# A four-stage fused kernel: copies and grid products regrouped in the attention stage, and a new end of the last image

## The chip, the cores and the metric

The kernel runs on one core of a Trainium2 chip. The metric is the device time of one execution in microseconds (us), and lower is better. Three executions of the kernel before took 2770.07, 2771.0 and 2774.91 us; their median is 2771.0 us.

## The reference, cut to what matters

Four layers are applied one after the other to `x`, which holds 8 images of 512 rows and 512 columns, all in float32:

```python
# layer 0: a grid step; Af, Bf are x times coefficient grids, _grad/_grad2 are differences of neighbours
x = maximum(f + (-gradv_Af + gradvv_Bf * 0.5) * dt, 0)
# layer 1: attention with 16 heads of 32, a bias [8,16,512,512] and a key mask, then an MLP of 2048
x = _ln(src) * (1 + scale) + shift
q, k, v = x @ Wq + bq, x @ Wk + bk, x @ Wv + bv
probs = softmax(where(mask, -inf, q/sqrt(32) @ k.T + attention_bias))
x = x + (probs @ v @ Wo + bo);  h = _ln(x) * g2 + beta2
x = x + _gelu2(h @ W1 + b1) @ W2 + b2
# layer 2: one of 8 experts per image
o = gelu(x @ Wi[e] + bi[e]) @ Wo[e] + bo[e] + x
x = (o - mean(o)) * rsqrt(var(o) + 1e-12) * gamma[e] + beta[e]
# layer 3: a rank-32 response, scaled by one number per image
base_act = sigmoid(relu(x.mean(rows) @ gate_w1.T + gate_b1) @ gate_w2.T + gate_b2)
strength = base_act * sigmoid(safety_score)
x = x + strength * ((x @ basis) @ basis.T[:, :32] @ resp_w.T + resp_b + safety_bias)
```

The output is the `x` of the last line.

## The kernel before

The kernel is one program for one core. Nearly every instruction is put down through `pin`, which keeps the order of the program on its engine, so the order of each engine's queue is the order in which the Python text makes the instructions. An image is held as four tiles of 128 rows: row `4p + r` lies in partition `p` of tile `r`. TensorE is PE below, VectorE DVE, ScalarE ACT, GpSimd POOL.

**Attention stage** (`attention_stage`). The work of an image is cut into 16 units, one for each group `c` of four heads and each tile `r` of query rows; `t = 4c + r` is the step of the unit within its image, and the main loop runs through 128 units. In the step of a unit

- POOL adds the mask to the bias of the next unit (`add_mask`). A small `gate` instruction ahead of it makes it wait until the last grid product of the step before is done,
- PE turns the exponentials of the unit before (`turned`, pair `u` of heads, head `i` of the pair: four transposes into one PSUM tile of the tag `tr`, which has two buffers). DVE copies the tile out where `i` is 0 and ACT where `i` is 1 (L1022 and L1024),
- DVE takes bias minus score and its row minimum (`softmax`, L997) and ACT makes the exponential and its sum (L1002). The four score tiles have one buffer each, so the scores of the next unit wait for this unit's four minima,
- PE does a piece of projection work (`fill`): a block of Q, K or V, or of the output projection. A block is four matmuls in two halves, one after each pair's transposes. In step 9 it is a block of K (`k_block`), and behind it stand the 16 transposes of the next image's input (`x1_in`, four `xtr` tiles of the tag `tr`; DVE copies out tiles 0 and 2, ACT tiles 1 and 3),
- in every second step PE multiplies probabilities and V (`values`), and after the last unit of a head group it transposes the inverse sums (`divide`, tile `rb`, also of the tag `tr`), which ACT copies and DVE multiplies into the context (`ct`),
- DVE does some products of the grid step of a later image, at the end of the step. The dict `GRID` says which: `j` is the step of the grid work, and its image `n` is at `j = t + 8` where `n = b + 1` and at `j = t - 8` where `n = b + 2`. So in each image steps 0 to 8 hold `j = 8` to 16 and steps 8 to 15 hold `j = 0` to 7. What stands in front of a `|` is done ahead of `divide`, the rest behind it. The last image's steps have no grid work, since no image follows.

SP issues the loads of bias tiles (8 buffers) and of grid coefficients (2 and 3 buffers) in the order of the text.

**MLP stage** (`mlp_stage`). Sixteen products `q`: 0 to 7 are the MLP of layer 1, 8 to 15 the experts, each as a Strassen scheme with seven products per level. `run(q, hooks)` counts steps `s`; `hooks` puts other work (loads, the norm and transposes of the next image, the layer-3 end of the image before) in front of step `s`. `second(s, ...)` makes one of the seven products of the second level: 16 matmuls of 128x256 into one PSUM tile, for two tiles of rows at once. The seventh, at steps 52 to 55, gives the left 256 columns of row tiles 2 and 3.

**The end of the last image** (`q = 15`). Row tiles 0 and 1 are complete early: their norm is at hook 49 (`tail_norm`), their transposes in front of steps 51 to 54 (`tail_turn`, L1167 and L1624), and the projection `tail_feats` and the product with gamma (`tail_gamma`, L1604) in front of step 55. After step 55 everything for row tiles 2 and 3 follows: addition, two `bn_stats`, power on POOL, two scalings (L85), eight transposes in pairs with ACT copies, the rank-32 projection `pf` alternating with the gate product `pg`, `h1` in two DVE instructions, then `po` for four row tiles (weights `rw`, then `ones` times the bias row `rb`), then `strength` (`pz`, a sigmoid on ACT, a product on DVE), then four sums on DVE (`tail_add`, L1683) and two stores from SP (L1688).

Of the kernel before, what the change touches and what calls it, by code (L numbers as in the profile page):

```python
# [544 lines left out]
def attention_stage(  # L545
# [13 lines left out]
    with ExitStack() as ctx:  # L559
# [85 lines left out]
            )  # L645
            qs[b, c] = t

        def k_block(b, c, tag="m"):
            pr = ps.tile([P, S], F32, name=f"pk_{b}_{c}", tag=tag)
            half = block(  # L650
                pr, lambda k: w["Wk"][:, k, c * P : (c + 1) * P], lambda k: x1s[b, k]
            )
            yield half(0)
            yield half(1)
            t = pp.tile([P, S], F32, name=f"kt_{b}_{c}", tag="kt")
            pin(nc.scalar.activation(t, pr, AF.Identity, bias=bqk[:, 1, c : c + 1]))
            ks[b, c] = t

        def v_block(b, m, tag="m", bufs=1):
            pr = ps.tile([P, D], F32, name=f"pv_{b}_{m}", tag=tag, bufs=bufs)  # L660
# [98 lines left out]
        def grid_op(n, op):  # L759
# [59 lines left out]


        GRID = {
            0: "q0 q1", 1: "e0 |", 2: "w0 c0 hh", 3: "C0", 4: "+0 -0", 5: "g0 |", 6: "G0 a0",
            7: "A0 b0 B0", 8: "x0 q2", 9: "e1 | w1 c1", 10: "C1 +1", 11: "-1 g1", 12: "G1 s0",
            13: "a1 | n0 A1 b1", 14: "B1 x1", 15: "s1", 16: "n1",
        }

# [81 lines left out]
        def fill(b, t):  # L908

            n = b + 1  # L910
            jobs = []
            if b == 0:
                if t == 0:
                    homes = (("m", 1), ("tr", 2), ("tr", 2), ("ctx", 1))
                    for m in range(4):
                        jobs.append(v_block(0, m, *homes[m]))
                        jobs.append(grid_early(j) for j in (m + 3,))
                    jobs.append(grid_early(7) for _ in range(1))
                    jobs.append(mask_out(0, r) for r in (2, 3))
                elif t == 2:  # L920
                    jobs.append(add_bv() for _ in range(1))
                elif t in (3, 4, 6, 7):
                    jobs.append(x1_back(0, (3, 4, 6, 7).index(t)) for _ in range(1))
            if t in (0, 4, 8):
                jobs.append(q_block(b, t // 4 + 1))
            elif t in (1, 5, 9):
                jobs.append(k_block(b, t // 4 + 1))
            elif t in (2, 3, 6, 7):
                if b:
                    jobs.append(o_block(b - 1, (2, 3, 6, 7).index(t)))  # L930
            elif n < NB:
                if t == 11:
                    jobs.append(q_block(n, 0))
                elif t == 13:
                    jobs.append(k_block(n, 0))
                else:
                    jobs.append(v_block(n, (10, 12, 14, 15).index(t)))
            if n < NB:
                if t == 9:
                    jobs.append(x1_in(n, c) for c in range(KC))  # L940
                if t in (11, 12, 13, 14):
                    jobs.append(x1_back(n, t - 11) for _ in range(1))
                if t >= 12:
                    jobs.append(load_mask(n, t - 12) for _ in range(1))
            elif t == 8:
                jobs.append(head_stats() for _ in range(1))
            elif t in (10, 11):
                jobs.append(head_norm(r) for r in (2 * t - 20, 2 * t - 19))
            elif t >= 12:
                jobs.append(head_turn(t - 12) for _ in range(1))  # L950
            for j in jobs:
                yield from j
# [55 lines left out]
        def turned(b, c, r, u):  # L1008

            bt = bias.pop((b, c, r, u))  # L1010
            for i in range(2):
                h = 2 * u + i
                if r % 2 == 0:
                    pts[b, c, r // 2, h] = pp.tile(
                        [P, KC, 2, P], F32, name=f"pt_{b}_{c}_{r}_{h}", tag=f"pt{h}", bufs=1
                    )
                pt = pts[b, c, r // 2, h]
                tr = ps.tile([P, KC, P], F32, name=f"tr_{b}_{c}_{r}_{h}", tag="tr", bufs=2)
                for k in range(KC):
                    tp(tr[:, k, :], bt[:, i, k * P : (k + 1) * P])  # L1020
                if i == 0:
                    pin(nc.vector.tensor_copy(pt[:, :, r % 2, :], tr))  # L1022
                else:
                    pin(nc.scalar.copy(pt[:, :, r % 2, :], tr))  # L1024
# [111 lines left out]
def mlp_stage(tc, a, small, xp, io, wo8, x1d, ident, eidx, sigs, layernorm, rstd_of, phalf, wl3, g2, b1, first):  # L1136
# [19 lines left out]
    with ExitStack() as ctx:  # L1156
# [297 lines left out]
        def run(q, hooks):  # L1454
# [119 lines left out]
            add(yu, p7, yu)  # L1574
            x_add(1, 1, yu)
            x_add(1, 0, yu)
            p4 = second(52, lambda g: act_quad(g, 1, 1), b(1, 0))
            x_add(1, 0, p4)

        def t13(q, g):  # L1580

# [46 lines left out]
                )  # L1628
                t["ys"][c] = y

        def tail_feats(q, rows):
            ys = outs[q]["ys"]
            pf = ps.tile([P, P], F32, name=f"pf_{q}_{rows[0]}", tag="tr")
            for c in range(KC):
                for i, r in enumerate(rows):
                    mm(
                        pf[r * RK : (r + 1) * RK, :], wl3[:, c, :], ys[c][:, i, :],
                        c == 0, c == KC - 1,
                    )
            m = slice(rows[0] * RK, (rows[-1] + 1) * RK)  # L1640
            pin(nc.vector.tensor_copy(outs[q]["ft"][m, :], pf[m, :]))

        def gate(q):

            pooled = outs[q]["pooled"]
            if len(pooled) > 1:
                add(pooled[0], pooled[0], pooled[1])
            pg = ps.tile([P, 1], F32, name=f"pg_{q}", tag="tr")
            for c in range(KC):
                mm(pg, gw1[:, c, :], pooled[0][:, c : c + 1], c == 0, c == KC - 1)  # L1650
            h1 = small.tile([P, 1], F32, name=f"h1_{q}", tag="h1")
            pin(nc.vector.tensor_scalar(h1, pg, 1.0 / S, gb1, ALU.mult, ALU.add))
            pin(nc.vector.tensor_scalar(h1, h1, 0.0, None, ALU.max))
            outs[q]["h1"] = h1
# [13 lines left out]
            gadd(x, x, beta[:, None, :].to_broadcast([P, R, D]))  # L1668

        def tail_sum(q, r):  # L1670
            last = q == NQ - 1
            ft, m = outs[q]["ft"], slice(r * RK, (r + 1) * RK)
            po = outs[q]["po", r] = ps.tile(
                [P, D], F32, name=f"po_{q}_{r}", tag="u", bufs=6
            )
            mm(po, ft[m, :], rw[m, :], True, not last)
            if last:
                mm(po, ones[m, :], rb[m, :], False, True)

        def tail_add(q, r):  # L1680
            x, t = xs[q], outs[q]
# [5 lines left out]
            if r % 2:  # L1687
                nc.sync.dma_start(  # L1688
                    a["out"][q - NB].rearrange("(p r) f -> p r f", r=R)[:, r - 1 : r + 1, :],
                    x[:, r - 1 : r + 1, :],  # L1690
                )


# [10 lines left out]
        for q in range(NQ):  # L1704
# [50 lines left out]
            if q == NQ - 1:  # L1755
                half = range(0, 2)
                at(hooks, 49, tail_norm, q, half)
                for c in range(KC):
                    at(hooks, 51 + c, tail_turn, q, half, [c])
                at(hooks, 55, tail_feats, q, half)  # L1760
                at(hooks, 55, tail_gamma, q, half)
            run(q, hooks)

        q, half = NQ - 1, range(2, 4)
        x, beta, t = xs[q], extra[q][1][2], outs[NQ - 1]
        gadd(x[:, 0:2, :], x[:, 0:2, :], beta[:, None, :].to_broadcast([P, 2, D]))
        tail_norm(q, half)
        pg = ps.tile([P, 1], F32, name=f"pg_{q}", tag="u", bufs=6)
        for c in range(KC):
            mm(pg, gw1[:, c, :], t["pooled"][0][:, c : c + 1], c == 0, False)  # L1770
        tail_turn(q, half, range(KC))
        tail_gamma(q, half)
        pf = ps.tile([P, P], F32, name=f"pf_{q}_2", tag="u", bufs=6)
        for c in range(KC):
            for i, r in enumerate(half):
                mm(
                    pf[r * RK : (r + 1) * RK, :], wl3[:, c, :], t["ys"][c][:, i, :],
                    c == 0, c == KC - 1,
                )
            mm(pg, gw1[:, c, :], t["pooled"][1][:, c : c + 1], False, c == KC - 1)  # L1780
        m = slice(half[0] * RK, (half[-1] + 1) * RK)
        h1 = small.tile([P, 1], F32, name=f"h1_{q}", tag="h1")
        pin(nc.vector.tensor_copy(t["ft"][m, :], pf[m, :]))
        pin(nc.vector.tensor_scalar(h1, pg, 1.0 / S, gb1, ALU.mult, ALU.add))
        pin(nc.vector.tensor_scalar(h1, h1, 0.0, None, ALU.max))
        t["h1"] = h1
        gadd(x[:, 2:4, :], x[:, 2:4, :], beta[:, None, :].to_broadcast([P, 2, D]))
        for r in range(R):
            tail_sum(q, r)
        strength(q)  # L1790
        for r in range(R):
            tail_add(q, r)


# [86 lines left out]
```

## Time and profile before

| what | value |
|---|---|
| median of three executions | 2771.0 us |
| the profiled execution, by its own time | 2773.14 us |
| its span from the first to the last instruction | 2771.4 us |
| PE, DVE, ACT, POOL busy | 2708.5, 1941.1, 1004.9, 1501.9 us |
| scores of the first unit to those of the last | about 70 to 1104 us |
| first matmul of the MLP stage to the last one of step 55 | 1132 to 2749 us |
| from there to the end of the span | 22.4 us |

A busy PE is not a PE at full speed: ends of matmuls are modelled, and a matmul that waits behind its own first half counts as busy. So times between the same marks of different images are compared below, not busy shares alone. The profiled execution is 2.1 us above the median of the three.

### The profile page before, as it was taken

What the parts mean: (1) busy time and instruction counts of PE and PEld (TensorE: products, weight loads), DVE (VectorE), ACT (ScalarE), POOL (GpSimd) and SP (SyncE); (2) the same over time, 40 slices, a digit from 0 to 9 for tenths busy, and PEclk for the clock granted to TensorE, in tenths of its full rate; (3) what the DMA queues carried; (4) which work ended last, traced back from release to release, by engine and by line L of the source; (5) the groups of instructions that cost most, each with busy time, mean ns of one, the idle gap of its engine ahead of it and who ended that gap; (6) DMA issues with size and microseconds to landing.
All of it is one profiled execution on the core that took longest, in us unless ns stands there. A gap on an engine that the chain in (4) does not pass through costs nothing.

```text
span 2771.4 us, 39819 instructions
## 1 busy us (share of the span) xinstructions
PE 2708.5 (98%) x14662; PEld 2009.6 (73%) x14662; DVE 1941.1 (70%) x3581; ACT 1004.9 (36%) x2137; POOL 1501.9 (54%) x1074
## 2 busy tenths in 40 slices
PE   7899999999999999999999999999999999999998
PEld 4455555555555554788888888888888888888886
DVE  7889898988888756577667666755456566566564
ACT  2566666666666666212111211211121221221221
POOL 3455555555555654466465555655636646646643
PEclk9999999999999999999999999999999999999998
DMA  8665757666666555542542543344133143142120
GB/s 317 234 208 169 240 179 238 192 219 214 193 231 193 162 155 171 173 114 65 160 126 40 154 134 85 101 145 133 58 126 114 58 156 114 58 156 99 59 76 31
DMA packets 190208, 405.27 MB, mean 146 GB/s; under 512 B 24024, under 2 KB 28704, under 8 KB 183742
## 3 DMA queue, kind: packets, MB, share of 16 engines
q1 hardware_dynamic: 186202, 391.97, 42.5%
q0 software_dynamic: 3360, 10.68, 3.1%
q8 instruction: 117, 1.92, 0.3%
q14 instruction: 77, 0.63, 0.1%
q10 hardware_dynamic: 452, 0.07, 0.0%
HBM read 366.97 MB, written 31.50 MB: 144 GB/s over the span
## 4 chain that ended last, share of the span: by engine, by line
PE 86%; DVE 10%; ACT 3%; DMA 1%; issue 1%; SPq 0%; ACTq 0%; POOL 0%; DVEq 0%
PE u L1164 28%; PE y L1164 28%; PE tr L570 7%; PE s L567 4%; PE ctx L567 4%; PE o L567 3%; PE pv L567 3%; PE pq L567 3%; PE pk L567 2%; DVE bt L997 2%; DVE x L687 2%; DVE pt L1022 1%; ACT bt L1002 1%; PE btr L1167 1%; PE ytr L1167 1%
## 5 line engine op out<-in xcount | busy, mean ns | idle before, releaser
L974 POOL TENSOR_TENSOR bt<-bt,mk 128x1024 f32<-128x1024 f32 x256 | 542.7, 2142 | 64.1 <-DMA bt<-in_bias 59.1
L1164 PE MATMUL y<-wo,act 128*128 128x256 f32 x2560 | 573.2, 380 | 0.0
L1164 PEld LDWEIGHTS y<-wo,act 128*128 128x128 f32 x2560 | 481.3, 190 | 70.0 <-issue 6.9
L1002 ACT ACTIVATE bt<-bt,mn 128x512 f32<-128x512 f32 x512 | 365.5, 715 | 112.1 <-DVE mn L997 112.1
L570 PEld LDWEIGHTS tr<-ident,bt 128*128 128x128 f32 x2048 | 228.1, 141 | 169.6 <-issue 116.8
L1164 PE MATMUL u<-bt,wi 128*128 128x256 f32 x1440 | 330.5, 379 | 0.0
L997 DVE CUSTOM_DVE_ANT_0 bt<-s,bt 128x512 f32<-128x512 f32 x512 | 330.5, 683 | 0.0
L1170 DVE TENSOR_TENSOR act<-u,u 128x512 f32<-128x512 f32 x256 | 173.3, 686 | 210.0 <-PE u L1164 132.3
L1164 PEld LDWEIGHTS u<-bt,wi 128*128 128x128 f32 x1440 | 273.5, 190 | 37.2
L570 PE MATMUL tr<-ident,bt 128*128 128x128 f32 x2048 | 280.4, 278 | 20.3 <-DVE pt L1022 8.5
L1022 DVE COPY pt<-tr 128x512 f32<-128x512 f32 x256 | 175.9, 687 | 113.0 <-PE tr L570 112.8
L1164 PE MATMUL u<-tb,ws 128*128 128x256 f32 x1024 | 242.2, 379 | 0.0
L1164 PE MATMUL y<-t,s 128*128 128x256 f32 x1024 | 234.2, 380 | 0.0
L1024 ACT COPY pt<-tr 128x512 f32<-128x512 f32 x256 | 148.3, 579 | 183.3 <-PE tr L570 181.2
L1164 PEld LDWEIGHTS u<-tb,ws 128*128 128x128 f32 x1024 | 194.3, 190 | 26.6 <-DVE tb L1170 0.2
L1173 POOL TENSOR_TENSOR t<-wo,t 128x512 f32<-128x512 f32 x64 | 104.5, 1648 | 200.1 <-PE y L1164 200.0
L1164 PEld LDWEIGHTS y<-t,s 128*128 128x128 f32 x1024 | 191.1, 190 | 24.1
L1484 ACT ACTIVATE act<-act,b 128x512 f32<-128x512 f32 x128 | 82.9, 711 | 292.8 <-DVE act L1170 292.8
L1484 ACT ACTIVATE act<-act,bi 128x512 f32<-128x512 f32 x128 | 83.8, 712 | 282.6 <-DVE act L1170 282.6
L567 PE MATMUL s<-kt,qt 32*128 32x512 f32 x1024 | 171.5, 644 | 2.2 <-DVE mn L997 1.4
L1170 DVE TENSOR_TENSOR x<-y,x 128x512 f32<-128x512 f32 x96 | 64.5, 685 | 154.2 <-PE y L1164 100.3
L1170 DVE TENSOR_TENSOR u<-u,u 128x512 f32<-128x512 f32 x192 | 131.2, 684 | 57.4 <-PE u L1164 57.3
(317 smaller groups left out, 4261.0 us busy)
## 6 DMA issues: line engine op xcount, KB each, us to landing
bt<-in_bias SPq DMA_DIRECT2D x256, 512.0 KB
wo<-in_W SPq DMA_DIRECT2D x32, 1024.0 KB
wi<-in_Wi SPq DMA_DIRECT2D x32, 1024.0 KB
wo<-in_Wo_e SPq DMA_DIRECT2D x32, 1024.0 KB
wi<-in_W SPq DMA_DIRECT2D x28, 1024.0 KB
gq<-coef_q SPq DMA_DIRECT2D x21, 512.0 KB
x1d<-x SPq DMA_DIRECT2D x8, 1024.0 KB
x<-x1d SPq DMA_DIRECT2D x8, 1024.0 KB
```

The lines of the kernel that those rows point to most:

```text
L567: pin(nc.tensor.matmul(out, lhsT=lhsT, rhs=rhs, start=start, stop=stop))
L570: pin(nc.tensor.transpose(out, src, ident))
L687: pin(nc.vector.tensor_tensor(out, x, y, op))
L974: nc.gpsimd.tensor_tensor(bt, bt, mask[b, r][:, None, :].to_broadcast([P, 2, S]), ALU.add)
L997: nc.vector.tensor_tensor_reduce(bt[:, i, :], ss[h], bt[:, i, :], -1.0, 3.0e38, ALU.add, ALU.min, mn)
L1002: nc.scalar.activation(bt[:, i, :], bt[:, i, :], AF.Exp, bias=mn, scale=-1.0, accum_out=sums[b, c, r][:, h : h + 1],)
L1022: pin(nc.vector.tensor_copy(pt[:, :, r % 2, :], tr))
L1024: pin(nc.scalar.copy(pt[:, :, r % 2, :], tr))
L1164: pin(nc.tensor.matmul(out, lhsT=lhsT, rhs=rhs, start=start, stop=stop))
L1170: pin(nc.vector.tensor_tensor(out, x, y, op))
L1173: pin(nc.gpsimd.tensor_tensor(out, x, y, op))
L1484: nc.scalar.activation(acts[g][:, k, :], acts[g][:, k, :], func, bias=bi[:, j : j + 1])
```

## The change

Four edits.

1. *Copies.* In `turned`, the copy of the first head of the first pair moves from DVE to ACT for five of the 16 units of every image: the units 1, 3, 5, 7 and 15, which are turned in steps 2, 4, 6, 8 and in step 0 of the next image.
2. *Grid products.* Six products of `GRID` stand one step earlier (`w0`, `C0`, `+0`, `g0`, `A0` by one step each, and `G0`, now ahead of the `|`). Those of `j = 8` to 16 stay.
3. *Transposes of the next input.* The 16 transposes of step 9 no longer follow the block of K: tiles 0 and 1 stand in front of its fourth matmul, tiles 2 and 3 behind the copy of the block.
4. *The end.* The seventh product of `q = 15` is made row tile by row tile (8 matmuls of one tile, then 8 of the other), and each tile's sum, statistics and scaling follow on their own. The transposes of row tiles 0 and 1 stand in front of steps 51, 52 and 53 (two). `tail_feats` of tiles 0 and 1, the four bias products (`ones`, `rb`) and the first half of `pg` stand behind the last product, ahead of the last transposes. `h1` is one ACT instruction. `pz` stands ahead of the four `rw` products. The last sums: DVE takes row tiles 1 to 3, ACT scales tile 0 and POOL adds it, and each row tile has its own store, three of them from ACT's queue and one from SP's.

```diff
-        def k_block(b, c, tag="m"):
+        def k_block(b, c, tag="m", turn=None):
             pr = ps.tile([P, S], F32, name=f"pk_{b}_{c}", tag=tag)
-            half = block(...)
-            yield half(0)
-            yield half(1)
+            for k in range(KC):
+                mm(pr, w["Wk"][:, k, c * P : (c + 1) * P], x1s[b, k], k == 0, k == KC - 1)
+                if k == 1 or k == (2 if turn else 3):
+                    yield
+                if turn and k == 2:
+                    turn(0)
+                    turn(1)
             t = pp.tile([P, S], F32, name=f"kt_{b}_{c}", tag="kt")
             pin(nc.scalar.activation(t, pr, AF.Identity, bias=bqk[:, 1, c : c + 1]))
+            if turn:
+                turn(2)
+                turn(3)
...
         GRID = {
-            0: "q0 q1", 1: "e0 |", 2: "w0 c0 hh", 3: "C0", 4: "+0 -0", 5: "g0 |", 6: "G0 a0",
-            7: "A0 b0 B0", 8: "x0 q2", 9: "e1 | w1 c1", 10: "C1 +1", 11: "-1 g1", 12: "G1 s0",
+            0: "q0 q1", 1: "e0 | w0", 2: "c0 hh C0", 3: "+0", 4: "-0 g0", 5: "G0 |", 6: "a0 A0",
+            7: "b0 B0", 8: "x0 q2", 9: "e1 | w1 c1", 10: "C1 +1", 11: "-1 g1", 12: "G1 s0",
             13: "a1 | n0 A1 b1", 14: "B1 x1", 15: "s1", 16: "n1",
...
-                jobs.append(k_block(b, t // 4 + 1))
+                turn = (lambda c: x1_in(n, c)) if t == 9 and n < NB else None
+                jobs.append(k_block(b, t // 4 + 1, turn=turn))
...
-                if i == 0:
+                if i == 0 and not (u == 0 and 4 * c + r in (1, 3, 5, 7, 15)):
                     pin(nc.vector.tensor_copy(pt[:, :, r % 2, :], tr))
                 else:
                     pin(nc.scalar.copy(pt[:, :, r % 2, :], tr))
...
+            else:                                    # q == NQ - 1
+                for m in range(2):
+                    y = ps.tile([P, H], F32, name=f"y_{q}_52_{m}", tag="u", bufs=6)
+                    for g in range(NG):
+                        if g % 2 == 0:
+                            go(52 + 2 * m + g // 2)
+                        for i in range(2):
+                            mm(y, act_quad(g, 1, 1)[:, i, m * P : (m + 1) * P],
+                               b(1, 0)(g)[:, i, :], g + i == 0, g + i == NG)
+                    last_row(m, y)
...
+        def last_row(m, y):
+            o = x[:, r, 0:H]
+            add(o, y, o)
+            pin(nc.vector.bn_stats(st, x[:, r, :]))
+            pin(nc.vector.bn_aggr(mv, st))
+            rs = z["rs", r] = rstd_of(mv[:, 1:2], LN_EPS2, 1, "ln2", pin)
+            if m == 0:
+                tail_gamma(q15, [0, 1])
+                scaled()
+                return
+            last_turn(0)
+            tail_feats(q15, range(0, 2), "u", 6)
+            for k in range(R):
+                mm(po, ones[k * RK : (k + 1) * RK, :], rb[k * RK : (k + 1) * RK, :], True, False)
+            for c in range(KC):
+                mm(pg, gw1[:, c, :], t["pooled"][0][:, c : c + 1], c == 0, False)
+            scaled()
+            gadd(x[:, 0:2, :], x[:, 0:2, :], beta[:, None, :].to_broadcast([P, 2, D]))
+            last_turn(1)
+            for c in range(KC):      # ACT: copies of the transposes of tiles 2 and 3, with column sums
...
+            tail_gamma(q15, [2, 3])
+            gadd(x[:, 2:4, :], x[:, 2:4, :], beta[:, None, :].to_broadcast([P, 2, D]))
+            for c in range(KC):      # pf of tiles 2 and 3, and pg, in turn
...
+            pin(nc.scalar.activation(h1, pg, AF.Relu, bias=gb1, scale=1.0 / S))
+            pin(nc.vector.tensor_copy(t["ft"][2 * RK :, :], pf[2 * RK :, :]))
+            strength(q15)
+            for r in range(R):
+                mm(t["po", r], t["ft"][m, :], rw[m, :], False, True)
+            pin(nc.scalar.mul(v, t["po", 0], t["st"]))
+            for r in (1, 2, 3):
+                pin(nc.vector.scalar_tensor_tensor(
+                    x[:, r, :], t["po", r], t["st"], x[:, r, :], ALU.mult, ALU.add))
+                if r == 1:
+                    gadd(x[:, 0, :], x[:, 0, :], v)
+                pin((nc.sync, nc.scalar)[r % 2].dma_start(out[:, r, :], x[:, r, :]))
+                if r == 2:
+                    pin(nc.scalar.dma_start(out[:, 0, :], x[:, 0, :]))
...
                 for c in range(KC):
-                    at(hooks, 51 + c, tail_turn, q, half, [c])
-                at(hooks, 55, tail_feats, q, half)
-                at(hooks, 55, tail_gamma, q, half)
+                    at(hooks, (51, 52, 53, 53)[c], tail_turn, q, half, [c])
```

The lines that stood behind `run(q, hooks)` for the last image are removed; their order is told above.

## The prediction

> **What bounds the kernel now.** I read the page first, then times by step, then the order of time inside single steps.
>
> ```profile
> span 2771.4 us, 39819 instructions
> PE 2708.5 (98%) x14662; PEld 2009.6 (73%) x14662; DVE 1941.1 (70%) x3581; ACT 1004.9 (36%) x2137; POOL 1501.9 (54%) x1074
> PE 86%; DVE 10%; ACT 3%; DMA 1%; issue 1%; SPq 0%; ACTq 0%; POOL 0%; DVEq 0%
> ```
>
> PE is the bound, yet a tenth of the chain that ended last runs through DVE. Where? The MLP stage is shut: from 1400 to 2740 us PE is busy for 1339.77 of 1340 us, and nothing there changes. What is left is the attention stage and the end. Steps 0 to 8 of an image hold the same PE work in every image from image 1 on, but in the last image, 7, they hold no grid products. Their time in image 2 (first line) and in image 7:
>
> ```profile
> 346.77:417.40 70.63, 68.80 (x425) 36.30 (x424) 64.98 (x136) 44.65 (x110) 40.54 (x28) 1.00 0.58 182
> 991.93:1057.92 65.99, 65.99 (x426) 35.41 (x425) 40.44 (x106) 43.14 (x108) 34.02 (x16) 1.00 0.55 175
> ```
>
> The columns are length, then busy time of PE, PEld, DVE, ACT, POOL, then clock and DMA. At the same clock and with the same matmuls the steps with grid products take 4.64 us more. DVE is 92% busy in them, ACT 63%. Only 1.83 us of the 4.64 shows as idle PE; the rest hides in scores that take longer. Step 2 shows how (PE, DVE, ACT, POOL in turn):
>
> ```profile
> 366.32 0.60 PE L570 MATMUL tr<-ident,bt 128*128 128x128 f32 x4
> 367.73 0.66 PE L570 MATMUL tr<-ident,bt 128*128 128x128 f32 x4 [0.81 <-DVE pt L1022]
> 370.04 1.85 PE L567 MATMUL s<-kt,qt 32*128 32x512 f32 x8
> ...
> 365.86 1.22 DVE L687 TENSOR_TENSOR gc<-gc,gf 128x1024 f32<-128x1024 f32 x1
> 366.99 0.69 DVE L1022 COPY pt<-tr 128x512 f32<-128x512 f32 x1
> 371.32 1.36 DVE L687 TENSOR_TENSOR x<-x,gc 128x1024 f32<-128x1024 f32 x1
> ...
> 365.07 0.58 ACT L1024 COPY pt<-tr 128x512 f32<-128x512 f32 x1
> ...
> 367.36 4.23 POOL L974 TENSOR_TENSOR bt<-bt,mk 128x1024 f32<-128x1024 f32 x2
> ```
>
> DVE leaves step 1's grid products at 366.99, only then copies the first transposes, and frees their buffer at 367.7; PE waits 0.81. All minima come later too, and the next scores take 1.85 us instead of 1.14. ACT has been idle since 365.65. In step 6 the wait ends elsewhere:
>
> ```profile
> 399.11 1.26 PE L570 MATMUL tr<-ident,bt 128*128 128x128 f32 x8 [0.70 <-ACT pt L1024]
> 396.98 1.52 ACT L814 ACTIVATE x<-x,gsh,grs 128x512 f32<-128x512 f32 x2
> 398.40 0.56 ACT L1024 COPY pt<-tr 128x512 f32<-128x512 f32 x1
> ```
>
> There ACT itself is late, behind the two norm instructions of the grid work.
>
> **Edit 1, the copies.** Forty DVE copies of 0.69 become ACT copies of 0.57. Per image the stalls against image 7 are, by step (the step's excess, with the scores that open the next step): 0: 0.51 + 0.21; 2: 1.02 + 0.71; 4: 0.18 + 0.21; 6: 1.10 + 0.71; 8: 0.17; in all 4.82. What goes:
> - Step 2: ACT would copy at 365.07 and 365.65 and be done at 366.2, before PE asks at 366.3; the wait is gone. DVE's minima start 0.6 earlier; the second pair's end near where the scores need them, and I leave 0.45 of stall. Gain 1.28.
> - Step 6: both copies stand behind the norms, at 398.40 and 398.96, so the transposes start at 399.1 as before: 0.70 and its refill stay. DVE, a copy lighter, gives the minima 0.6 earlier: gain 0.71.
> - Steps 0, 4 and 8: DVE's wait (0.32 in step 0) and late scores go: 0.72 + 0.39 + 0.17.
>
> Sum 3.27 per image. Behind the moved copies in ACT's queue stand the exponentials, which wait for DVE's minima and come after the copies anyway: no cost. In image 7, where DVE isn't late, the second copy ends 0.2 later; the next transposes come 1.7 later, so nothing, but 0.2 at the stage's very end.
>
> A rule speaks against this. The row: `x<-x,gc` takes 1.36 where the same product takes 1.22 alone, and POOL's mask addition ends at 371.59, 0.27 into it. The Trainium skill (SBUF — State Buffer, Who interferes with whom) says that a DVE instruction with two SBUF inputs and a GpSimd one that reads SBUF block each other fully, whoever comes second. By it a DVE that is early by a copy gains nothing for its products: `gc` is held to 371.59 whenever it comes, since POOL's `gate` ties that addition to the step before. By the row alone it would start earlier for 0.14. I take the block: products then end when they end now, PE arrives up to 1.3 earlier and meets DVE later by that much. Step 3 opens with 1.9 us of `ctx` before its transposes, which absorbs it. If it did not, steps 3 and 7 would give back up to 1.3 and 0.7, leaving 1.3 per image.
>
> **Edit 2, grid products.** Nothing removed; each moved one is 1.2 to 1.36. Step 15 gets one fewer, so step 0 opens with DVE 1.2 less late (in 0.72 above). Step 9 gets `w0` behind `divide`: DVE starts step 10 about 1.2 later, its copy ends at 0.3 before PE needs the buffer, its last minimum about when the scores want it: 0 to 0.1. The `gate` of step 10 waits for `w0`, so POOL's additions move by 1.2 to 2.2, with 3 us to spare before their minima. Coefficient loads keep their SP places; `g0` is issued some 20 us before its new use. Steps 10 to 15 show no stall now. I take 0, bounded by +0.5 and -0.3 per image.
>
> **Edit 3, transposes of the next input.**
>
> ```profile
> 298.27 1.34 PE L570 MATMUL xtr<-ident,x 128*128 128x128 f32 x8 [0.47 <-DVE x L612]
> 299.83 0.66 PE L570 MATMUL rb<-ident,rw 128*128 128x128 f32 x4 [0.22 <-DVE x L612]
> ```
>
> PE reaches `rb` at 299.83. In the new order tile 0 starts at 295.5, when DVE's copy (295.46) frees the buffer; tile 1 ends at 296.5 and matmul 4 at 296.9; DVE is through its minima at 296.67 and copies tile 0 by 297.5; tile 2 follows to 298.1, DVE's next copy ends 298.95, `rb` starts 299.0. ACT does tile 1 right behind its exponentials (297.57), ahead of the K copy. Gain 0.8, for seven images.
>
> Attention: 6 x (3.27 + 0.8) = 24.4 for images 1 to 6. Image 0 has other work in these steps (`x1_back`); its PE waits add up to 8 us from 105 to 231 us, and I give the copies 2 of them, so 2.8 with edit 3. Less 0.2 at the end: 27.0.
>
> **Edit 4, the end.** Stations of before, by PE, DVE and SP:
>
> ```profile
> 2746.99 1.99 PE L1164 MATMUL y<-wo,act 128*128 128x256 f32 x8
> 2753.18 1.27 PE L1167 MATMUL ytr<-ident,x 128*128 128x128 f32 x4 [3.40 <-DVE x L85]
> 2763.78 0.38 PE L1164 MATMUL pz<-h,gw 128*128 128x1 f32 x2
> 2764.76 2.73 DVE L1683 SCALAR_TENSOR_TENSOR x<-po,st,x 128x512 f32<-128x512 f32 x4
> ```
>
> - Last product: the projection of tiles 0 and 1 (1.07 and a wait of 0.2) leaves the front; step 52 still starts at 2740.28. 32 instructions at 0.219 (48 took 10.5) and two transposes give 2748.0 instead of 2748.98. Tile 2's sum starts at 2744.5 and runs beside tile 3's product: 0.4 + 0.69 + 0.2 + 0.2, the gamma product 1.23 (over the power, 0.71), scaling 0.5, done 2747.8.
> - Behind 2748.0 PE does four transposes 0.76, the projection 1.07, four bias products (half of the 3.5 that eight took: 1.75; in separate row groups 1.14, as eight instructions took at 2725.91), `pg` 0.95. DVE needs to 2750.9 for tile 3, so PE is last: transposes at 2751.5 to 2752.3, against 2753.18.
> - Only four transposes, no buffer wait, ACT from 2752.2 at 0.55 each; `pf`/`pg` in the old pitch of 1.09: `pg` ends 2757.3 instead of 2760.41.
> - `h1` on ACT 0.26 (its nearest row is the sigmoid of 128x1), no table load ahead of it in the program. `pz` at 2757.6, since six of the eight `po` passes no longer stand before it: 6.2 earlier than 2763.78. Sum ready 0.98 later as before, 2758.6; `rw` products about 2758.9.
> - Three DVE sums of 0.68 end 2760.95; ACT's scaling (0.58, as its copies) and POOL's addition (1.27 at 2717.26; at most 1.65) end about 2760.9. The last store leaves ACT's queue near 2761.3; the last one now leaves at 2767.54 and the span ends 3.8 later. Gain 6.2 to 6.3.
>
> New here and without a row: stores from ACT's queue, behind POOL's addition (nearest SP's, 0.34 to issue; 0 to 1 us worse). I take 6.3, between 4 and 7.5.
>
> **Sum.** 27.0 + 6.3 = 33.3. The profiled execution would go from 2773.14 to 2739.8; against the median of 2771.0, 2.1 lower, 2737.7. I say 2738.
>
> **Rivals.**
> - *The late DVE comes back in the next step.* The block above takes edit 1 down to 1.3 per image; with 0.8 that is 12.6, image 0 gives 1.5, the end 6: 20, so 2751. For it: DVE is still over 85% busy and its products share the port with 4.2 us of POOL per step. Against: odd steps have 0.6 to 1.1 us of DVE slack each. 0.20.
> - *More stalls go than I count*: steps 2 and 6 fully (1.5 more per image), image 0 by 5 more: 2724. Against: ACT's norms in step 6 stay. 0.10.
> - *The end gains, the attention stage doesn't*, since products moved into step 9 open a new wait there as large as those removed: 2765. 0.04.
> - *ACT becomes the one that PE waits for* (the other side). Forty copies of 0.57 ahead of exponentials; if each holds back the transposes of its step by its whole length and a late exponential holds the next step's too, 46 us come in, the stalls of now stay, and the end gives 6: 2811. It decides where ACT reaches the copies later than DVE does now: in step 2 it is 1.3 us earlier, in step 6 0.6. 0.03.
> - *The edits do not do what they say*: were ACT's copies scheduled elsewhere, 0.01; the order of the changed program shows them in place.
>
> **How the numbers follow.** The likeliest case, 0.62, spans 2732 to 2746. The range adds the first rival to 2751 and some of the second: 2730 to 2752. Differences within 0.2% (5.5 us) can't be told from none here. Faster 0.94, same 0.03, slower 0.03.
>
> **What would show it.** Steps 0 to 8 of images 1 to 6 should take about 67.5 instead of 70.6 us, step 2 without PE idle, step 6 still with some 0.7 behind ACT; step 9 about 11.2 instead of 12.0; from the last product to the span's end 17 instead of 22.4 us. Wrong would be: longer scores in steps 1, 3 and 7, a new wait in step 10, or ACT as releaser in steps 2 and 4.

## The result, and the profile after

The changed kernel takes 2753.07 us (median of 4 executions, 2751.5 to 2755.17), the kernel before 2772.95 beside it (4 executions): ratio 0.9929, interval 0.9912 to 0.9946. It is faster by 20 us, where 33 were forecast; 2752 was the upper end of the range.

The page after, with the lines that answer to those of before (span, busy time, chain):

```profile
span 2751.2 us, 39879 instructions
PE 2696.8 (98%) x14662; PEld 2006.6 (73%) x14662; DVE 1933.4 (70%) x3540; ACT 1024.9 (37%) x2179; POOL 1504.7 (55%) x1076
PE 90%; DVE 6%; ACT 2%; DMA 1%; issue 1%; SPq 0%; ACTq 0%; POOL 0%; DVEq 0%
```

DVE's share of the chain fell from 10 to 6%. Steps 0 to 8 of image 2 (first line) and of image 7, columns as before (length; busy PE, PEld, DVE, ACT, POOL; clock; DMA share and rate):

```profile
341.56:410.34 68.78, 67.95 (x426) 36.10 (x425) 62.80 (x131) 47.38 (x115) 40.53 (x28) 1.00 0.60 188
973.16:1039.15 65.99, 65.99 (x426) 35.41 (x425) 37.46 (x101) 44.98 (x112) 34.14 (x16) 1.00 0.55 174
```

70.63 became 68.78, where 67.5 was forecast; the floor of 65.99 is as it was. The two profiled executions differ by 20.2 us (2773.14 to 2752.93): image 0 gave 2.6, images 1 to 6 gave 2.7 each (129.0 to 126.3), image 7 with the end of the attention stage 0.45, the MLP nothing. The stretch from the start of step 52 to the end of the span went from 31.08 to 30.0. So two places fell short: the images with grid products, by 1.4 each, and the end, by 5.2.

In step 2 PE no longer idles. First the last minimum of step 2 in the kernel before, then PE, DVE and POOL of the changed kernel:

```profile
370.02 0.69 DVE L997 CUSTOM_DVE_ANT_0 bt<-s,bt 128x512 f32<-128x512 f32 x1
...
360.39 1.04 PE L570 MATMUL tr<-ident,bt 128*128 128x128 f32 x8
361.27 1.88 PE L567 MATMUL o<-Wo,ct 128*128 128x512 f32 x4
363.08 2.28 PE L567 MATMUL s<-kt,qt 32*128 32x512 f32 x8
363.49 0.69 DVE L1004 CUSTOM_DVE_ANT_0 bt<-s,bt 128x512 f32<-128x512 f32 x1
364.79 1.96 DVE L695 TENSOR_TENSOR x<-x,gc 128x1024 f32<-128x1024 f32 x1
361.43 4.23 POOL L981 TENSOR_TENSOR bt<-bt,mk 128x1024 f32<-128x1024 f32 x2
```

The transposes follow without a wait, yet the scores of step 3 now take 2.28 instead of 1.85 (1.14 without a wait). PE reaches them 1.03 earlier within the step, which starts at 362.60 before and at 356.68 now. The last minimum they wait for (370.02 before, 363.49 now) starts only 0.60 earlier, so the scores wait 0.43 longer. Step 6 keeps its wait (PE, then ACT):

```profile
392.53 1.06 PE L570 MATMUL tr<-ident,bt 128*128 128x128 f32 x8 [0.75 <-ACT pt L1031]
390.40 1.52 ACT L822 ACTIVATE x<-x,gsh,grs 128x512 f32<-128x512 f32 x2
391.83 1.04 ACT L1031 COPY pt<-tr 128x512 f32<-128x512 f32 x2
```

The end, in the order PE, DVE, POOL, ACT's queue:

```profile
2733.68 0.66 PE L1174 MATMUL ytr<-ident,x 128*128 128x128 f32 x4 [0.92 <-DVE x L1727]
2739.36 2.09 PE L1171 MATMUL po<-rw,ft 32*128 32x512 f32 x8
2731.07 2.56 DVE L1727 TENSOR_SCALAR x<-x,z_mv,ln_r 128x512 f32<-128x512 f32 x1
2731.01 2.34 POOL L1180 TENSOR_TENSOR x<-x,beta 128x1024 f32<-128x1024 f32 x1
2742.29 1.27 POOL L1180 TENSOR_TENSOR x<-x,z_r 128x512 f32<-128x512 f32 x1 [4.26 <-ACT z_r L1782]
2744.05 0.41 ACTq L1791 DMA_DIRECT2D out<-x  x1
```

Tile 3's scaling takes 2.56 where tile 2's takes 0.55. The `rw` products (eight instructions) take 2.09 at a granted clock of 0.5, which begins at 2736.2; the eight bias products of the same shape take 1.14 at 1.0. The last store leaves at 2744.05. Each engine's queue closes with a DRAIN instruction, which the views leave out; in the trace's records SP is through at 2747.14, but POOL's DRAIN lasts until 2750.35. The final records of all engines follow 0.2 behind it.

### The profile page after: what moved, and what is told of

The parts are those of the page before. It is cut to its first block, busy times and chain, and to the rows that moved or that the text cites. A ratio compares the mean times of both kernels' runs of the same rounds, so it can differ in the third digit from the quotient of the medians.

```text
span 2751.2 us, 39879 instructions
## 1 busy us (share of the span) xinstructions
PE 2696.8 (98%) x14662; PEld 2006.6 (73%) x14662; DVE 1933.4 (70%) x3540; ACT 1024.9 (37%) x2179; POOL 1504.7 (55%) x1076
## 4 chain that ended last, share of the span: by engine, by line
PE 90%; DVE 6%; ACT 2%; DMA 1%; issue 1%; SPq 0%; ACTq 0%; POOL 0%; DVEq 0%
PE u L1171 28%; PE y L1171 28%; PE tr L570 8%; PE s L567 5%; PE ctx L567 4%; PE pq L567 4%; PE pv L567 3%; PE o L567 3%; PE pk L567 3%; PE btr L1174 1%; ACT bt L1009 1%; DVE x L695 1%; DVE bt L1004 1%; PE ytr L1174 0%; DVE pt L1029 0%
## 5 line engine op out<-in xcount | busy, mean ns | idle before, releaser
L1031 ACT COPY pt<-tr 128x512 f32<-128x512 f32 x296 | 167.9, 581 | 167.5 <-PE tr L570 164.4
L1029 DVE COPY pt<-tr 128x512 f32<-128x512 f32 x216 | 148.5, 688 | 99.3 <-PE tr L570 88.0
L1177 DVE TENSOR_TENSOR x<-y,x 128x512 f32<-128x512 f32 (+1 forms) x97 | 64.7, 680 | 155.8 <-PE y L1171 101.9
```

Source lines behind the costliest of these rows:

```text
L1177: pin(nc.vector.tensor_tensor(out, x, y, op))
```

## The experiments

The executions of one kernel differ by 4 to 5 us in all, in part by where stretches of half clock fall: step 11 of the last image took 8.43 without one and 11.58 with 6.8 us of it. Image 0 varies too: in four traces with the same attention stage (the changed kernel and three with another end) it took 142.1 to 145.3. So runs of one execution are read by step times and stations, not by their totals. Step times repeat to 0.02 us from image to image (single images of some runs stray by some tenths, one step by 2.1). Lengths of steps in us, from the first score to the next step's, the usual value of images 2 to 6:

| kernel | 0+1 | 2+3 | 4+5 | 6+7 | 9 | image |
|---|---|---|---|---|---|---|
| before | 15.83 | 16.41 | 15.51 | 16.47 | 11.99 | 129.0 |
| changed | 15.12 | 15.82 | 15.12 | 16.33 | 11.20 | 126.3 |
| edit 1 undone | 15.11 | 16.41 | 15.51 | 16.47 | 11.30 | 127.6 |
| edit 2 undone | 15.24 | 15.81 | 15.12 | 16.33 | 11.20 | 126.4 |
| two copies more on ACT | 15.11 | 15.22 | 15.12 | 16.32 | 11.19 | 125.7 |
| unit 3's copy back | 15.11 | 15.82 | 15.51 | 15.99 | 11.20 | 126.4 |
| unit 5's copy back | 15.12 | 15.82 | 15.11 | 16.81 | 11.14 | 126.7 |
| norms behind step 6 | 15.11 | 15.81 | 15.12 | 17.66 | 11.87 | 128.3 |
| two copies more, half a mask | 15.11 | 15.22 | 15.11 | 15.92 | 11.14 | 125.3 |
| image 7 (no grid products) | 15.11 | 14.68 | 15.12 | 14.67 | 8.71 | |

**Edit 1 undone.**

```diff
-                if i == 0 and not (u == 0 and 4 * c + r in (1, 3, 5, 7, 15)):
+                if i == 0:
```

> The changed kernel with edit 1 undone: all first copies of a pair on DVE again. Step times, scores to scores, images 1 to 6 (changed kernel: steps 2+3 6.41+9.41, steps 6+7 7.64+8.69, steps 0 to 8 together 68.8). Theory SUM: in steps 2 to 3 and 6 to 7 DVE has more work than PE, and the scores of steps 3 and 7 wait for its last minimum; a copy taken from it is worth its own 0.6 and no more, wherever the waits of PE are seen. Then without the copies steps 2+3 take about 16.4 instead of 15.82, steps 0+1 and 4+5 together 0.4 to 0.8 more, steps 6+7 0.15 to 0.3 more; steps 0 to 8 about 70.1. Theory PORT (the first rival of the prediction: what the copies free is taken by the product that waits for POOL's mask addition): steps 2+3 keep 15.8.

Steps 2 to 8 went back to the times of before, to 0.02. Steps 0+1 did not, against the expectation: edit 2 alone holds them at the floor. Taken out alone, the five copies are worth 1.3 per image, not 3.27, and 0.59 in steps 2+3. That is one copy's place in DVE's queue: its record reads 0.69, but in the kernel before DVE's next instruction begins 0.60 after it (366.99 to 367.59). Step 9 took 11.30 instead of 11.20, since its opening scores are late again (1.30 instead of 1.20).

**Edit 2 undone.**

```diff
-            0: "q0 q1", 1: "e0 | w0", 2: "c0 hh C0", 3: "+0", 4: "-0 g0", 5: "G0 |", 6: "a0 A0",
-            7: "b0 B0", ...
+            0: "q0 q1", 1: "e0 |", 2: "w0 c0 hh", 3: "C0", 4: "+0 -0", 5: "g0 |", 6: "G0 a0",
+            7: "A0 b0 B0", ...
```

> The changed kernel with edit 2 undone: the six grid products back in their old steps. The prediction gave edit 2 nothing but a product less in front of step 0. Theory SUM: DVE enters step 0 later by one product of 1.2 less what slack step 15 has; steps 0+1 0.2 to 0.5 longer than 15.12, steps 1 to 8 as they are, steps 9 and 10 within 0.1. Rival (edit 2 is worth nothing): no step moves by more than 0.1.

Steps 0+1 lose 0.12, less than expected, and nothing else moves. With the run above: either edit alone takes most of the late start of step 0 away (0.72 by edit 2, 0.59 by the copies), and the two overlap.

**Two copies more on ACT** (units 1 and 5, second pair).

```diff
-                if i == 0 and not (u == 0 and 4 * c + r in (1, 3, 5, 7, 15)):
+                if i == 0 and not (4 * c + r in ((1, 3, 5, 7, 15), (1, 5))[u]):
```

> The changed kernel with two copies more on ACT: the first head of the second pair of units 1 and 5, which are turned in steps 2 and 6. Theory SUM: 0.6 less for DVE ahead of the last minima of steps 2 and 6, so the scores of steps 3 and 7 end sooner: step 3 8.8 instead of 9.41, step 7 8.3 to 8.4 instead of 8.69 (its floor is 8.27), about 1.0 per image. Rival ACT: the copies stand between two pairs of exponentials on ACT and hold them back, PE then waits for ACT in steps 3 and 7: gain 0.3 or less, and waits on the exponentials in the view of waits. Rival PORT: the product of step 3 is held to the end of POOL's addition, and step 3 keeps 9.3 to 9.4.

Step 3 took 8.81, as expected: one more copy, 0.60 more. Step 7 kept 8.69 against the expectation. Its lines (PE, DVE, POOL, ACT):

```profile
392.94 1.14 PE L567 MATMUL s<-kt,qt 32*128 32x512 f32 x8
399.33 0.66 PE L570 MATMUL tr<-ident,bt 128*128 128x128 f32 x4 [0.20 <-ACT pt L1031]
393.74 2.04 DVE L695 TENSOR_TENSOR x<-x,gb 128x1022 f32<-128x1022 f32 x1
390.47 4.23 POOL L981 TENSOR_TENSOR bt<-bt,mk 128x1024 f32<-128x1024 f32 x2
398.69 0.59 ACT L1031 COPY pt<-tr 128x512 f32<-128x512 f32 x1 [0.29 <-ACT x L802]
```

The scores are short now (1.14). But the product `x<-x,gb` ends at 395.78, 1.08 behind POOL's addition; a ReLU on ACT waits for it by way of one more DVE instruction, and the copy that PE needs stands behind the ReLU.

**Half a mask.** On top of the two copies, one of the two mask additions of step 6 is left out.

```diff
-            for u in range(2):
+            for u in range(1 if b and (c, r) == (1, 3) else 2):
```

> The kernel with two copies more on ACT, with one of the two POOL mask additions of step 6 left out in images 1 to 7 (half of the mask of unit 7 is not added, so this part of the result is not the reference's). Theory PORT: the grid product x*gb of step 7 ends 1.08 behind POOL's last mask addition whenever it starts (372.68 behind 371.59 in the kernel before, 395.78 behind 394.70 with more copies), so in step 7 the time won from a copy is lost to POOL. With POOL done 2.1 earlier the product takes 1.22 instead of 2.04, the ReLU and ACT's copy behind it come 0.8 earlier and step 7 falls from 8.69 to 8.27-8.35; steps 0 to 6 stay. Rival: the product is slow by its own shape (1022 of 1024 elements, shifted rows) and step 7 stays at 8.69.

DVE and POOL of step 7:

```profile
392.40 1.19 DVE L695 TENSOR_TENSOR x<-x,gb 128x1022 f32<-128x1022 f32 x1
389.12 2.14 POOL L981 TENSOR_TENSOR bt<-bt,mk 128x1024 f32<-128x1024 f32 x1
```

The same product takes 1.19, and step 7 takes 8.27, the floor. This shows that POOL's addition holds a DVE product with two SBUF inputs, and that in the kernel with two copies more this is what lengthens step 7.

**The norms behind step 6.**

```diff
-            13: "a1 | n0 A1 b1", 14: "B1 x1", 15: "s1", 16: "n1",
+            13: "a1 | A1 b1", 14: "B1 x1 n0", 15: "s1", 16: "n1",
```

> The changed kernel with the two norm instructions (n0) at the end of step 6 instead of the end of step 5, so that ACT reaches the copies of step 6 with nothing in front. Theory SUM: PE's wait of 0.75 in step 6 goes (step 6 6.6 to 6.9 instead of 7.64), but the last minimum of step 6 comes as late as before and the scores of step 7 wait for it instead: step 7 9.2 to 9.5 instead of 8.69, steps 6+7 within 0.2 of 16.33. Rival (ACT's norms set steps 6 and 7): step 7 stays at 8.7 and steps 6+7 fall by 0.8 to 1.0.

Step 6 fell to 6.71 and the scores of step 7 took 2.32 (1.45 in the changed kernel), so the wait moved as theory SUM says. But step 7 came to 10.95, not 9.2 to 9.5:

```profile
395.25 2.32 PE L567 MATMUL s<-kt,qt 32*128 32x512 f32 x8
403.90 0.66 PE L570 MATMUL tr<-ident,bt 128*128 128x128 f32 x4 [1.28 <-ACT pt L1031]
401.86 1.52 ACT L822 ACTIVATE x<-x,gsh,grs 128x512 f32<-128x512 f32 x2 [0.30 <-DVE mn L1004]
```

On ACT the norms now stood behind the ReLU and in front of step 7's copies, which the expectation had overlooked: a new wait of 1.28.

**Unit 3's copy back, unit 5's copy back.** One of the five copies each returns to DVE.

```diff
-... in (1, 3, 5, 7, 15)):
+... in (1, 5, 7, 15)):     # unit 3's, turned in step 4; the other run: (1, 3, 7, 15)
```

> The changed kernel with one copy of edit 1 back on DVE: unit 3's, which is turned in step 4. All five copies together brought 0.39 in steps 4+5 (15.12 instead of 15.51) and 0.14 in steps 6+7 (16.33 instead of 16.47). Theory ONE CHAIN: from step 4 to the last minimum of step 6 it is one DVE queue, of which PE waits once, at the scores of step 7; a stall that goes in steps 4 and 5 only lets PE come earlier to the next wait. Then without this copy steps 4+5 lose up to 0.39 and steps 6+7 win back part of it: steps 4 to 7 together at most 0.2 longer than 31.45. Theory ADD (the prediction's sum): steps 4+5 0.39 longer and steps 6+7 as they are, together 31.84.

> The changed kernel with unit 5's copy, which is turned in step 6, back on DVE. Theory ONE CHAIN: DVE's last minimum of step 6 comes 0.6 later, PE's transposes in step 6 0.15 sooner (ACT has one copy less behind its norms): step 6 about 7.5, step 7 9.1 to 9.3, together 16.6 to 16.8 instead of 16.33, although all five copies together brought only 0.14 here. Theory ADD (a copy brings in its own step what the table of steps shows for it): steps 6+7 go back to 16.47.

Steps 4+5, then 6+7, of image 2, columns as above: before, changed, unit 3's back, and steps 6+7 alone with unit 5's back:

```profile
379.02:394.52 15.50, 15.50 (x101) 8.38 (x100) 15.27 (x33) 8.95 (x25) 9.43 (x7) 1.00 0.47 141
394.52:411.00 16.48, 15.78 (x98) 8.04 (x97) 14.52 (x31) 11.45 (x27) 7.96 (x6) 1.00 0.50 165
...
372.49:387.60 15.11, 15.11 (x101) 8.21 (x100) 14.64 (x32) 9.20 (x26) 9.46 (x8) 1.00 0.49 149
387.60:403.93 16.33, 15.50 (x97) 7.91 (x97) 14.71 (x30) 12.03 (x28) 7.47 (x6) 1.00 0.50 154
...
372.36:387.87 15.51, 15.51 (x102) 8.37 (x101) 15.26 (x33) 8.97 (x25) 9.46 (x8) 1.00 0.47 146
387.87:403.85 15.98, 15.28 (x97) 7.93 (x96) 14.43 (x30) 11.68 (x27) 7.46 (x6) 1.00 0.50 157
...
388.74:405.55 16.81, 15.99 (x97) 8.02 (x96) 14.78 (x31) 11.78 (x28) 7.96 (x6) 1.00 0.49 161
```

With unit 3's copy back, steps 4+5 lose 0.40 and steps 6+7 win 0.35 back: together 31.49 instead of 31.44. So the 0.39 that the change shows in steps 4 and 5 is worth 0.05; it lets PE come earlier to step 6, where it waits for the same DVE and ACT work as before. Unit 5's copy is worth 0.48 in its steps (16.81 against 16.33), though the change as a whole shows 0.14 there. Together that is the 0.53 by which steps 4 to 7 became shorter. Theory ONE CHAIN holds. Step 6 alone took 7.83 in that run, not the 7.5 expected.

**The end without POOL.** Tile 0's last sum becomes a fourth one on DVE.

```diff
-            v = ap.tile([P, D], F32, name="z_r", tag="tmp", bufs=4)
-            pin(nc.scalar.mul(v, t["po", 0], t["st"]))
-            for r in (1, 2, 3):
+            for r in range(R):
...
-                if r == 1:
-                    gadd(x[:, 0, :], x[:, 0, :], v)
```

> The changed kernel with row tile 0's last sum on DVE as well, as a fourth sum: no ACT scaling and no POOL addition at the end. Theory DRAIN: POOL's closing DRAIN ends 6.79 us after POOL's last operation (before 2759.75 to 2766.54, hidden behind the stores; after 2743.56 to 2750.35, in the open). Here POOL ends with the beta addition at about 2738.0, its DRAIN at 2744.8, ahead of SP's. The last store is issued at about 2744.4, SP's own closing follows 3.1 later: from the start of step 52 to the end of the span 27.0 us instead of 30.0, the whole about 3 us less. Rival: the closing waits for the stores from ACT's queue and POOL's record only shows that wait; then the end stays at 29.5 to 30.5.

DVE, POOL and ACT's queue:

```profile
2744.84 2.73 DVE L1783 SCALAR_TENSOR_TENSOR x<-po,st,x 128x512 f32<-128x512 f32 x4 [1.60 <-PE po L1171]
2738.57 2.34 POOL L1180 TENSOR_TENSOR x<-x,beta 128x1024 f32<-128x1024 f32 x1 [2.34 <-DVE x L1624]
2746.32 1.68 ACTq L1787 DMA_DIRECT2D out<-x  x2
```

POOL ends at 2740.92 and its DRAIN at 2747.71, 6.79 later; SP's, at 2750.47, comes last. The last store leaves 0.7 later than in the changed kernel, counted from the last product's end (16.1 and 15.4), and yet the span ends 2.8 earlier (19.7 instead of 22.5). So the sum on POOL costs 2.8. Against a run with the changed kernel's end whose clock fell as early as here (unit 3's copy back: 22.9) it is 3.2, as much as POOL's DRAIN outlasts SP's in the changed kernel. Why the DRAIN lasts so long is open.

**A POOL addition at the end of the kernel before.**

```diff
         for r in range(R):
             tail_add(q, r)
+        z = small.tile([P, 1], F32, name="z_end", tag="h1")
+        gadd(z, x[:, 3, 0:1], x[:, 3, 0:1])
```

> The kernel before with one 128x1 POOL addition behind its last sum (it reads one column of x and writes a scratch tile). Theory DRAIN: the addition ends near 2767.8, POOL's DRAIN 6.8 later, so the span ends near 2775.4 instead of 2771.4: from the start of step 52 to the end 35 us instead of 31.1. Rival (the DRAIN follows the stores): 31.1 to 31.5.

```profile
2764.89 0.19 POOL L1173 TENSOR_TENSOR z_end<-x 128x1 f32<-128x1 f32 x1 [8.40 <-DVE x L1683]
```

It ends at 2765.08, the DRAIN at 2771.87: 6.79 again. From the last product to the span's end it is 26.9 instead of 22.4; 0.5 of the 4.5 is a later last store (the clock fell 2.5 behind the last product, before 4.2), the rest the DRAIN. In the kernel before the DRAIN ran from POOL's last addition (2759.75) to 2766.54, covered by SP, which was through with the stores at 2770.57.

**The beta addition earlier.**

```diff
+            if m == 0:
+                tail_gamma(q15, [0, 1])
+                gadd(x[:, 0:2, :], x[:, 0:2, :], beta[:, None, :].to_broadcast([P, 2, D]))
             o = x[:, r, 0:H]
             add(o, y, o)
```

> The changed kernel with the gamma product and the beta addition of row tiles 0 and 1 ahead of row tile 2's addition, in the 2 us in which DVE is idle, so that POOL is free when tile 3 is scaled. Theory PORT: the 2.56 us of tile 3's scaling are POOL's beta addition (2731.01 to 2733.35) that holds DVE up; here the scaling takes 0.55, tile 2's power 0.56 instead of 1.46, and the last transposes start when PE has done its first half of pg, about +11.2 behind the start of step 52 instead of +12.5; the last store leaves about 1.3 earlier, and the span, still held by POOL's DRAIN, ends at 28.7 instead of 30.0. Rival: tile 3's scaling is long for another reason (it waits for the power through a long semaphore path); then +12.5 stays.

DVE's scaling of tile 3, then PE:

```profile
2734.40 0.55 DVE L1730 TENSOR_SCALAR x<-x,z_mv,ln_r 128x512 f32<-128x512 f32 x1 [0.48 <-POOL ln_r L71]
2735.48 0.63 PE L1174 MATMUL ytr<-ident,x 128*128 128x128 f32 x4
2740.06 1.14 PE L1171 MATMUL po<-rw,ft 32*128 32x512 f32 x8
```

The scaling takes 0.55, and the last transposes start 3.35 behind the last product instead of 5.01. The clock stayed full until 10.3 behind the last product (7.5 in the changed kernel), and from these transposes to the last store it took 8.3 instead of 10.4: the span ends 18.8 behind the last product instead of 22.5.

**Matmuls without a use in PE's gaps.**

```diff
+            for k in range(2):
+                mm(t["po", k], ones, rb, True, True)
...
+            for k in range(2):
+                mm(pf, ones, rb[:, 0:P], True, True)
```

> The changed kernel with four matmuls without a use in the gaps of PE near the end: two of 128x512 behind the first half of pg, ahead of the bias products (they write tiles that the bias products then overwrite), and two of 128x128 behind the last transposes. Theory CLOCK: the granted clock falls to 0.5 at 2736.2 because PE has had little to do in the microseconds before; with the extra work it stays at 1.0 up to the rw products, pg ends about 0.8 earlier and the rw products take 1.14 instead of 2.09; the span ends 1.5 to 2 us earlier. Rival: the clock falls at this place whatever PE does (its fall comes a few us behind the long matmuls of step 55), then the rw products keep 2.0 to 2.1 and the span ends up to 0.5 later.

```profile
2737.89 2.00 PE L1171 MATMUL po<-rw,ft 32*128 32x512 f32 x8
```

The clock fell 10.6 behind the last product instead of 7.5 and `pg` ran at full clock, but the `rw` products still took 2.00, and the span ended 22.15 behind the last product: 0.3 won. Since the clock stayed up as long in the run above without such matmuls, this run does not show that they hold it.

**What they point to, together.** No POOL sum, the earlier beta addition, unit 1's second copy on ACT, the last image's unit 15 on DVE again; the second kernel has also unit 5's second copy on ACT and `n0` ahead of `B1` in step 6.

> The changed kernel with what the runs so far point to: all four last sums on DVE (no POOL at the end), the gamma product and beta addition of row tiles 0 and 1 ahead of row tile 2's addition, one copy more on ACT (unit 1, second pair), and the last image's unit 15 copied by DVE as before the change. Theories SUM, DRAIN and PORT together: step 3 8.81 instead of 9.41 in six images and as much in image 0 (4.2 us), the end of the attention stage 0 to 1, the end 6 to 6.6 (last product to the span's end 16 instead of 22.5): 2741 to 2743. If the parts of the end overlap (the last store again waits for half-clock products), 2743 to 2745.

> As the kernel with the new end and one more copy, with unit 5's second copy on ACT too and the norms n0 at the end of step 6, ahead of the product and the ReLU of that step. Theory SUM: step 6 6.7 and step 7 about 9.0, together 15.7 instead of 16.33: 3.7 us less than the kernel without this, 2738 to 2739. Rival: ACT's norms and ReLU in front of step 7's copies cost what step 6 gains (as with the norms behind the ReLU, where step 7 took 10.95): 2742 or more.

2741.5 us (2741.22 to 2745.05, ratio to before 0.989, interval 0.9874 to 0.9907) and 2740.56 (2739.8 to 2741.32, ratio 0.9886, 0.987 to 0.9903). The first is as expected, some 10 to 12 below the changed kernel. The norms brought nothing: step 6 took 6.71 and step 7 9.63, together 16.34, so the rival's mechanism holds; its total, 2742 or more, was not reached.

## Why the prediction was wrong, point by point

- *Step 2, "Gain 1.28".* This step failed. The prediction itself said that DVE's minima start 0.6 earlier, and then took away both the whole wait at the transposes (1.02) and 0.26 of the late scores (0.71, of which it left 0.45). They were one lateness of DVE, seen at two places of PE's queue. The scores wait for the last minimum; that came 0.60 earlier, the scores grew by 0.43, and steps 2+3 gained 0.59. Longer scores in step 3 were a sign of being wrong that the prediction had named. Edit 1 undone and the copy added both show 0.6 per copy.
- *Step 6, "gain 0.71", and step 4, 0.39, summed.* This failed for the same reason over four steps: together steps 4 to 7 gained 0.53, not 1.10. Unit 3's copy is worth 0.05 and unit 5's 0.48. The wait behind ACT stayed (0.75), as said.
- *Step 8, 0.17:* 0.10 came, in step 9, whose opening scores went from 1.31 to 1.20. *Step 0, 0.72:* 0.72 came, but edit 2, whose part the prediction put under this term, brings it alone; the copies add nothing there.
- *Edit 3, 0.8:* of the 0.79 that step 9 lost, 0.10 is the scores just named, which leaves 0.69. The size is nearly right, though no run undoes edit 3 alone.
- So an image gained 2.65 where 4.07 was summed: 1.4 short, some 8 us over six images.
- *Image 0, 2.8:* 2.6, which is luck, since this image varies by 3 us from one execution to another. *End of the stage, -0.2:* +0.45 with image 7, from half-clock stretches that fell elsewhere: step 11 took 3.15 less, the stretch from the last scores to the MLP 2.14 more.
- *The block of products by POOL.* The row (1.36, ending behind POOL's addition) and the Trainium skill's rule (SBUF — State Buffer, Who interferes with whom) were rightly taken as a full block: in the traces of before, the changed kernel and the one with two copies more, all 82 products of the grid work that start inside a mask addition end 1.08 to 1.09 behind it. The first rival put the loss of steps 2 and 3 down to this block. There it costs nothing: one more copy taken from DVE still brought 0.60 in step 3. The rival's total (2751) was the nearest, but by luck, since another mechanism than it named brought the loss. In step 7 the block is next in line.
- *The end, 6.3:* 1.1 came. The last product ended 7.51 behind the start of step 52 (7.7 forecast). But the last store left 22.9 behind it instead of 21.0, and the span ended 7.1 behind that store instead of 3.8. Three terms failed. "DVE needs to 2750.9 for tile 3, so PE is last" left out POOL's beta addition beside tile 3's scaling: 1.7 at the transposes. "The `rw` products about 2758.9" were sized at full clock: they took 2.09. The "old pitch of 1.09" of `pf` and `pg`, on the other hand, was a row at half clock; the first two here came at a pitch of 0.65 at full clock. The sum mixed two clocks. And "the span ends 3.8 later" than the last store took SP's closing for the only one: POOL's DRAIN of 6.79, put behind a POOL addition that is now among the last instructions, cost 2.8. In the last kernel, without either POOL effect and with the clock up somewhat longer, the stretch from the last product to the span's end takes 16.1; 17 was forecast, 22.5 came.
- Right were the sign, the unchanged MLP, step 9, step 2 without idle PE and step 6 behind ACT.

## What to carry to other kernels

When one engine is late in a row of steps, its waits in PE's queue do not add up: ask how much earlier the last instruction comes that PE waits for, and count a removed instruction once, at its own place in the queue (0.60 here). Before a last operation is given to an engine, read that engine's closing in the records of before: in these traces one on GpSimd must end 3.7 to 4.0 us ahead of the last store's issue to stay covered (its 6.79 against SP's 2.8 to 3.1). A DVE product of two SBUF tiles put beside a GpSimd addition is costed by the end of the latter (1.08 behind it here).

## What the runs showed of the hardware that was not expected

- In all fifteen traces POOL's closing DRAIN ends 6.79 us behind POOL's last operation, for a 128x1 addition as for one of 128x1024.
- A `tensor_scalar` of 128x512 with one SBUF tile as input (tile 3's scaling) is held by a POOL addition like a product of two: 0.55 alone, 2.56 beside an addition of 2.34, ending 0.28 behind it. In the other order POOL is held: its power of 128x1 took 1.46 beside a DVE product that had begun 0.17 earlier, and 0.56 alone.
- At the end of the program the clock fell to 0.5 for 10 to 17 us. Eight executions share the changed kernel's end; there the fall came 5.0 to 7.6 behind the last long product and the end took 23.6 to 22.5, in this order: 0.4 us for each us of an earlier fall. For the two last kernels, whose ends are the same instructions, the falls came 5.2 and 8.3 behind and the ends took 18.0 and 16.1, so that this chance is worth 1 to 2 us here.
- In each trace all falls of the clock lie whole multiples of 3.413 us apart (to 0.03 us over the whole span), and the first lies elsewhere in each (53.2 to 56.5). The Trainium skill (TensorE: Matmul & The Clock Gate, Part 1: The HAM clock gate) has the activity window free-running, so that its phase varies from run to run; these falls agree with that. The grid alone does not settle which of its points brings the fall. In the run with the earlier beta addition and in the two last kernels PE does the same instructions at the same times up to 4.7 behind the last product, and the clock fell 10.3, 5.2 and 8.3 behind it. What PE activity would hold the clock up is left open.
